# One block of quarter matmuls per step in linear attention, attended values a step later, and denominators finished on ScalarE

## The chip, the cores and the metric

The kernel runs on one NeuronCore of a Trainium2 chip. The metric is the time of one execution on the device in microseconds (us). Five engines work side by side, each through its own instructions in order: TensorE (PE in the profile; its weight loads are shown as PEld), VectorE (DVE), ScalarE (ACT), GpSimd (POOL) and SyncE (SP), which issues most transfers. They wait for one another through semaphores. TensorE writes its results to PSUM, of which the kernel uses eight banks of 128 x 512 floats.

## The reference, cut to what matters

Eight sequences of 64 tokens and width 512 go through three residual blocks: cross attention to a context of 1601 tokens, a linear-attention layer with a feed-forward part, and a mixture of eight experts. The change concerns the linear attention, with 16 heads of width 64:

```python
def _phi(x, proj):
    return jax.nn.elu(x @ proj) + 1.0
h = _ln(x, g1, beta1)
q = _phi((h @ wq).reshape(b, s, H, DH), proj)
k = _phi((h @ wk).reshape(b, s, H, DH), proj)
v = (h @ wv).reshape(b, s, H, DH)
def step(carry, qkv_t):
    kv, ksum = carry
    q_t, k_t, v_t = qkv_t
    kv = kv + k_t[..., :, None] * v_t[..., None, :]
    ksum = ksum + k_t
    num = jnp.einsum('bhd,bhde->bhe', q_t, kv)
    den = jnp.einsum('bhd,bhd->bh', q_t, ksum) + 1e-06
    return ((kv, ksum), num / den[..., None])
...
attn = jnp.moveaxis(outs, 0, 1).reshape(b, s, H * DH) @ wo
x = x + attn
h2 = _ln(x, g2, beta2)
x = x + (jax.nn.gelu(h2 @ w1 + b1, approximate=False) @ w2 + b2)
```

The scan is causal: at a token, the sums run over that token and the ones before it.

## The kernel before, in words

All is in 32-bit floats. The 512 tokens are four tiles of 128 (`NT`), each with two sequences; the width is four chunks of 128 (`KC`). Instead of the scan the kernel forms, for each sequence and head, the 64 x 64 matrix of products between key features and query features, sets to zero what lies in the future, and multiplies by the values.

The linear-attention stage works on two heads at a time, so a projection has `nj` = 8 steps `j`. For each step there are these parts:

- `linear(j, "wq")` and `linear(j, "wk")` (line 671): four matmuls of 128 x 128 weights on 512 tokens, into a PSUM bank; the trace shows each matmul as two instructions, 8 in all. ScalarE copies the bank to `lin`.
- `features(j)` (line 687): the projection of width 64, as four matmuls (8 instructions) that each use a quarter, 64 x 64, of TensorE's array, into two banks. VectorE takes the minimum with 0, ScalarE the exponential, VectorE the sum with the positive part. The result `phi` has one buffer for `wq` and one for `wk`.
- `products(j)` (line 710): 16 quarter matmuls (32 instructions) of key features by query features into two banks, which VectorE multiplies by the causal mask into `masked`.
- `attend_j(j)` (line 735): four quarter matmuls with ones for the denominators (8 instructions) and 16 with the values (32 instructions), into two banks. VectorE adds 1e-6 to the denominators (line 761), takes the reciprocal of 128 x 512 elements (line 762) and multiplies the attended values into `a_t[:, j]` (line 764).

After them `output(t, js)` (line 784) adds, for token tile t, the steps `js` to the output projection: two instructions for each j, with `a_t` as weights. Each of the four tiles has its own bank until all eight j are in. Then `join(t)` (line 813) adds the residual and takes the statistics on VectorE and a square root on ScalarE, `normal(t)` (line 824) normalizes on VectorE, and `turn_h2(t)` (line 829) transposes the tile on TensorE and evicts four chunks, by turns on VectorE and ScalarE. `hidden(f, tokens)` (line 863) is the first matmul of the feed-forward part; the kernel runs `hidden(0)` on three tiles, then turns the last tile, then goes on. GpSimd adds the second bias and the residual once a tile is normalized (lines 884, 885).

The order of every engine's work is the order in which the program writes it (`manual_schedule`, line 96). What can move are the banks: `mm_bank` (projections, products, output tiles 0 and 1, turned tiles) and `acc_bank` (features, attended values, output tiles 2 and 3) have four each, and a new use waits until an old one is read. Weights come through a ring of 12 buffers; `need` (line 209) issues transfers on SyncE's queue ahead of their use, in an order fixed at the start.

Before the change a step of the loop is, on TensorE: `linear(j, "wq")`, `features(j - 1)` with `attend_j(j - 2)`, `linear(j, "wk")`, `products(j - 1)`. So quarter matmuls stand in two blocks of each step between full matmuls of 128 x 128. After the loop come `features(7)`, then pieces of the output projection with `attend_j(6)`, `products(7)` and `attend_j(7)` between them.

Of the kernel before, what the change touches and what calls it, by code (L numbers as in the profile page):

```python
# [15 lines left out]
F32 = mybir.dt.float32  # L16
AF = mybir.ActivationFunctionType
# [3 lines left out]
P = 128  # L21
B, S, D = 8, 64, 512
LK = 1601
NT = B * S // P
# [24 lines left out]
def perceiver_kernel(  # L49
# [22 lines left out]
    nc = tc.nc  # L72
    const = ctx.enter_context(tc.tile_pool(name="const", bufs=1))
# [10 lines left out]
    def mm_bank(name):  # L84
        return ps.tile([P, 512], F32, tag="mm", name=name)

    def acc_bank(name):
        return ps.tile([P, 512], F32, tag="acc", name=name)
# [120 lines left out]
    def need(*key):  # L209
        if key[0] not in ("ctxT", "ctx", "tail", "wv"):  # L210
            done(*[k for k in held if place[k] < place[key] - AHEAD + 1])
            issue_to(place[key] + 1 + AHEAD)
        else:
            issue_to(len(order))
        return streamed[key]
# [9 lines left out]
        nc.gpsimd.memset(rows, 0.0)  # L225
    eps = const.tile([P, 1], F32, name="eps")
    nc.gpsimd.memset(eps, LN_EPS)
    warm0 = const.tile([P, 1], F32, name="warm0")
    nc.scalar.activation(warm0, eps, AF.Sqrt)
    b2_bc = const.tile([P, D], F32, name="b2_bc")  # L230
# [434 lines left out]
    if True:  # L665
        a_t = la1.tile([P, H * DH // P, B * S], F32, name="a_t")

        nj = H * DH // P
        lin, phi, qk_banks, masked, sums = {}, {}, {}, {}, {}

        def linear(j, which):


            w = need(which, j // 4)
            bank = mm_bank(f"{which}_{j}")
            for c in range(KC):
                nc.tensor.matmul(  # L677
                    bank,
                    w[:, c, (j % 4) * P : (j % 4 + 1) * P],
                    h_t[:, c, :],  # L680
                    start=(c == 0),
                    stop=(c == KC - 1),
                )
            lin[which, j] = la2.tile([P, B * S], F32, tag=f"lin_{which}", name=f"lin_{which}_{j}")
            nc.scalar.copy(lin[which, j], bank)

        def features(j):

            pr = {which: acc_bank(f"pr_{which}_{j}") for which in ("wq", "wk")}
            for r in range(2):  # L690
                rows = slice(r * DH, (r + 1) * DH)
                for which, other in (("wq", r), ("wk", 1 - r)):
                    nc.tensor.matmul(
                        pr[which][other * DH : (other + 1) * DH, :],
                        proj2[rows, :],
                        lin[which, j][rows, :],
                        start=True,
                        stop=True,
                    )

            ex = {}
            for which in pr:
                ex[which] = la2.tile([P, B * S], F32, tag="ex", name=f"ex_{which}_{j}")
                nc.vector.tensor_scalar_min(ex[which], pr[which], 0.0)
                nc.scalar.activation(ex[which], ex[which], AF.Exp)
            for which in pr:
                phi[which, j] = la2.tile([P, B * S], F32, tag=f"phi_{which}", bufs=1, name=f"phi_{which}_{j}")
                nc.vector.scalar_tensor_tensor(phi[which, j], pr[which], 0.0, ex[which], ALU.max, ALU.add)

        def products(j):  # L710


            banks_ = [mm_bank(f"qk_{j}_{r}") for r in range(2)]
            for t in range(NT):
                for h in range(2):
                    cols = slice(t * P + h * S, t * P + (h + 1) * S)
                    for r in range(2):
                        rows = slice(r * DH, (r + 1) * DH)
                        nc.tensor.matmul(
                            banks_[r][h * S : (h + 1) * S, t * S : (t + 1) * S],  # L720
                            phi["wk", j][rows, cols],
                            phi["wq", j][rows, cols],
                            start=True,
                            stop=True,
                        )
            for r in range(2):
                m = masked[j, r] = la2.tile([P, NT, S], F32, tag="masked", name=f"masked_{j}_{r}")
                nc.vector.tensor_tensor(
                    m,
                    banks_[r][:, : NT * S].rearrange("p (t q) -> p t q", t=NT),  # L730
                    mask[:, None, :].to_broadcast([P, NT, S]),
                    ALU.mult,
                )

        def attend_j(j):

            both = [acc_bank(f"nd_{j}_{h}") for h in range(2)]
            for r in range(2):  # L740
                for h in range(2):
                    nc.tensor.matmul(
                        both[h][r * DH : (r + 1) * DH, NT * S :],
                        ones[h * S : (h + 1) * S, :DH],
                        masked[j, r][h * S : (h + 1) * S, :, :].rearrange("p t q -> p (t q)"),
                        start=True,
                        stop=True,
                    )
            for t in range(NT):
                for r in range(2):  # L750
                    for h in range(2):
                        nc.tensor.matmul(
                            both[h][r * DH : (r + 1) * DH, t * S : (t + 1) * S],
                            v_sb[h * S : (h + 1) * S, t, (2 * j + r) * DH : (2 * j + r + 1) * DH],
                            masked[j, r][h * S : (h + 1) * S, t, :],
                            start=True,
                            stop=True,
                        )
            rden = la2.tile([P, 2, NT * S], F32, tag="rden", bufs=1, name=f"rden_{j}")
            for h in range(2):  # L760
                nc.vector.tensor_scalar_add(rden[:, h, :], both[h][:, NT * S :], 1e-6)
            nc.vector.reciprocal(rden, rden)  # L762
            for h in range(2):
                nc.vector.tensor_tensor(
                    a_t[:, j, :].rearrange("p (t h q) -> p t h q", t=NT, h=2)[:, :, h, :],
                    both[h][:, : NT * S].rearrange("p (t q) -> p t q", t=NT),
                    rden[:, h, :].rearrange("p (t q) -> p t q", t=NT),
                    ALU.mult,
                )

        for j in range(nj):
            linear(j, "wq")
            if j > 0:
                features(j - 1)
            if j > 1:
                attend_j(j - 2)
            linear(j, "wk")
            if j > 0:
                products(j - 1)

        wo_r = [need("wo", r) for r in range(2)]
        wo_banks = {}
# [1 line left out]
        def output(t, js):  # L784
            if t not in wo_banks:
                wo_banks[t] = (mm_bank if t < 2 else acc_bank)(f"wo_{t}")
            for j in js:
                nc.tensor.matmul(  # L788
                    wo_banks[t],
                    a_t[:, j, t * P : (t + 1) * P],  # L790
                    wo_r[j // 4][:, j % 4, :],
                    start=(j == 0),
                    stop=(j == nj - 1),
                )

        features(nj - 1)

        warm2 = small.tile([P, 1], F32, tag="warm2", name="warm2")
        nc.scalar.activation(warm2, eps, AF.Sqrt)
        output(0, range(0, 3))  # L800
        attend_j(nj - 2)
        output(0, range(3, nj - 2))
        products(nj - 1)
        output(1, range(nj - 2))
        attend_j(nj - 1)
        output(2, range(nj // 2 + 1))
        for t in range(2):
            output(t, [nj - 2, nj - 1])


        h2n, h2_t = v_sb[:, :, :D], v_sb[:, :, D:]
# [12 lines left out]
        def normal(t, mv, std):  # L824
            rstd = small.tile([P, 1], F32, tag="rstd1", name=f"rstd_h2_{t}")
            nc.vector.reciprocal(rstd, std)  # L826
            nc.vector.tensor_scalar(h2n[:, t, :], xin[:, t, :], mv[:, 0:1], rstd, ALU.subtract, ALU.mult)
# [16 lines left out]
        of = join(0), join(1)  # L844
        for t in range(2):
            normal(t, *of[t])
        output(2, range(nj // 2 + 1, nj))
        of = join(2)
        output(3, range(nj // 2))
        normal(2, *of)  # L850
        turn_h2(0)
        turn_h2(1)
        output(3, range(nj // 2, nj - 2))
        turn_h2(2)
        output(3, range(nj - 2, nj))
        of = join(3)
        normal(3, *of)
    las.close()
# [226 lines left out]
    t = NT - 1  # L1085
# [688 lines left out]
```

## Time and profile before

| what | value |
|---|---|
| time, median of 3 runs (lowest to highest) | 633.23 us (633.15 to 633.51) |
| profiled execution, whole time | 633.73 us |
| its span, first to last instruction | 632.0 us |
| mean granted TensorE clock | 0.995 |
| TensorE busy, share of the span | 616.1 us, 97% |
| VectorE busy | 182.3 us, 29% |
| ScalarE busy | 121.0 us, 19% |
| GpSimd busy | 65.0 us, 10% |
| linear attention, first projection to the last turned tile | 172.3 to 283.7 us |

Times inside the span count from its first instruction. A line of the timeline gives the start, the length from the first start to the last end, the engine, the line of the kernel, the operation with `written<-read` tiles, the shape and the number of instructions merged; in brackets stands the engine's idle time before it and what ended it. Matmuls overlap: a full one of 512 columns is shown with some 0.59 us, though the next starts 0.43 us after it, so distances of starts tell more than lengths. The tile names are those of the program: `pr` features, `qk` products, `nd` attended values and denominators, `wo` the output projection, `tr_h` turned tiles, `v_sb` (whose memory the normalized tiles reuse), `hid` the feed-forward part.

### The profile page before, as it was taken

The numbers are of one execution on the slowest core, as the hardware profiler recorded it, in microseconds if no ns is written. First come the engines' busy times: TensorE is split into PE (matmuls) and PEld (weight loads), VectorE is DVE, ScalarE is ACT, GpSimd is POOL, SyncE is SP. The second block draws the span as 40 slices with busy tenths as digits, with TensorE's granted clock in tenths as the row PEclk, the third lists the DMA queues.
The fourth block names the chain that finished last, engine by engine and source line by source line (L and its number), as shares of the span: only waits on it lengthen the run. The fifth ranks groups of instructions, "written<-read, shape, count | busy, mean of one in ns | idle before, by whom it ended". The sixth has DMA issues, their size and how long they took to land. (4 is left out here: it accounts for less than half of the span.)

```text
span 632.0 us, 8729 instructions
## 1 busy us (share of the span) xinstructions
PE 616.1 (97%) x3572; PEld 349.1 (55%) x3572; DVE 182.3 (29%) x430; ACT 121.0 (19%) x226; POOL 65.0 (10%) x88
## 2 busy tenths in 40 slices
PE   8999999999999999999999999999999999999994
PEld 6543434343444444455444446967783757775793
DVE  4122323243326888670000026511311111101100
ACT  2241323230132122031011111301101101101110
POOL 4000000000000000050000003331310121301100
PEclk9999999999999999999999999999999999999998
DMA  8999999999511203030313221437890577784711
GB/s 334 418 423 423 422 423 422 425 426 417 239 61 64 71 2 135 1 132 1 117 33 117 67 100 68 170 94 256 298 346 0 189 281 284 296 311 146 296 19 17
DMA packets 23938, 131.81 MB, mean 209 GB/s; under 512 B 4373, under 2 KB 4373, under 8 KB 12489
## 3 DMA queue, kind: packets, MB, share of 16 engines
q1 hardware_dynamic: 19496, 122.36, 49.1%
q0 software_dynamic: 3280, 7.61, 4.8%
q10 hardware_dynamic: 1104, 1.07, 0.5%
q8 instruction: 38, 0.62, 0.4%
q14 instruction: 20, 0.16, 0.1%
HBM read 126.08 MB, written 4.94 MB: 207 GB/s over the span
## 5 line engine op out<-in xcount | busy, mean ns | idle before, releaser
L1271 PEld LDWEIGHTS up<-xgT,e_up 128*128 128x128 f32 x896 | 100.7, 192 | 4.5 <-ACT y_sb L1249 2.5
L1271 PE MATMUL up<-xgT,e_up 128*128 128x128 f32 x896 | 101.6, 276 | 1.0 <-PEq L1604 0.6
L1237 DVE TENSOR_TENSOR mid<-up,act 128x256 f32<-128x256 f32 x38 | 16.2, 425 | 151.0 <-ACT act L1235 149.5
L1285 PE MATMUL y<-e_wo,mid 128*128 128x512 f32 (+1 forms) x144 | 58.8, 547 | 0.0
L869 PE MATMUL hid<-v_sb,w 128*128 128x512 f32 (+2 forms) x144 | 56.6, 545 | 0.0
L890 PE MATMUL mlp<-w,hid_sb 128*128 128x512 f32 x112 | 51.0, 597 | 0.0
L456 PE MATMUL sc<-ctxT,pw_t 128*64 128x401 f32 (+1 forms) x256 | 46.7, 503 | 0.5 <-DMA ctxT<-in_ctx_T_dram 0.5
L517 PE MATMUL av<-ctx,eT 128*64 128x512 f32 x192 | 44.5, 596 | 0.2 <-DMA ctx<-in_ctx_dram 0.2
L869 PEld LDWEIGHTS hid<-v_sb,w 128*128 128x128 f32 x144 | 26.2, 190 | 29.1 <-issue 27.2
L1235 ACT ACTIVATE act<-up 128x256 f32<-128x256 f32 x38 | 14.6, 383 | 120.4 <-PE up L1271 97.5
L1285 PEld LDWEIGHTS y<-e_wo,mid 128*128 128x128 f32 x144 | 25.7, 190 | 20.5 <-issue 17.8
L1250 POOL DMA_INDIRECT out_dram<-y_sb,dst_late x12 | 18.3, 1526 | 168.2 <-ACT y_sb L1249 99.6
L890 PEld LDWEIGHTS mlp<-w,hid_sb 128*128 128x128 f32 x112 | 20.8, 190 | 23.5 <-issue 23.4
L456 PEld LDWEIGHTS sc<-ctxT,pw_t 128*64 128x64 f32 x256 | 17.8, 136 | 27.0 <-issue 25.4
L884 POOL TENSOR_TENSOR xin<-xin,b_bc 128x512 f32<-128x512 f32 x4 | 5.1, 1268 | 267.1 <-DVE rstd_h L826 263.8
L677 PE MATMUL wk<-h_t,wk 128*128 128x512 f32 x64 | 29.5, 604 | 0.0
L677 PE MATMUL wq<-h_t,wq 128*128 128x512 f32 x64 | 29.4, 602 | 0.0
L587 PE MATMUL v<-wv,h_t 128*128 128x512 f32 x64 | 29.2, 598 | 0.0
L788 PE MATMUL wo<-wo,a_t 128*128 128x512 f32 x64 | 28.9, 599 | 0.0
L938 DVE TENSOR_TENSOR xs<-mlp,xs 128x512 f32<-128x512 f32 x3 | 2.1, 691 | 86.6 <-PE mlp L890 86.6
L762 DVE RECIPROCAL rden<-rden 128x512 f32<-128x512 f32 x8 | 26.8, 3354 | 0.3
L517 PEld LDWEIGHTS av<-ctx,eT 128*64 128x64 f32 x192 | 13.3, 136 | 24.5 <-issue 23.2
(270 smaller groups left out, 621.0 us busy)
## 6 DMA issues: line engine op xcount, KB each, us to landing
e_up<-in_L_ffn_up_dram SPq DMA_DIRECT2D x32, 1024.0 KB, 6.9
ctx<-in_ctx_dram SPq DMA_DIRECT2D x24, 1024.0 KB, 15.2
ctxT<-in_ctx_T_dram SPq DMA_DIRECT2D x24, 802.0 KB, 13.9
e_wo<-in_L_ffn_wo_dram SPq DMA_DIRECT2D x16, 1024.0 KB, 15.6
w<-in_L_attn_w_dram SPq DMA_DIRECT2D x8, 1024.0 KB, 4.7
ctxT<-in_ctx_T_dram SPq DMA_DIRECT2D x8, 796.0 KB, 17.5
wv<-in_L_attn_wv_dram SPq DMA_DIRECT2D x2, 1024.0 KB, 13.6
wq<-in_L_attn_wq_dram SPq DMA_DIRECT2D x2, 1024.0 KB, 15.3
```

The costliest lines, as they stand in the source:

```text
L456: nc.tensor.matmul(sc[h * S : (h + 1) * S, :width], pw_t[:, c, (2 * t + h) * S : (2 * t + h + 1) * S], keys[h][:, c, :], start=(c == 0), s ...
L517: nc.tensor.matmul(av[h * S : (h + 1) * S, :], e_t[:, 4 * g + j, h * S : (h + 1) * S], rows[h][:, j, :], start=(g == 0 and j == 0), stop=F ...
L587: nc.tensor.matmul(bank, h_t[:, c, t * P : (t + 1) * P], wv_n[:, c, :], start=(c == 0), stop=(c == KC - 1))
L677: nc.tensor.matmul(bank, w[:, c, (j % 4) * P : (j % 4 + 1) * P], h_t[:, c, :], start=(c == 0), stop=(c == KC - 1),)
L762: nc.vector.reciprocal(rden, rden)
L788: nc.tensor.matmul(wo_banks[t], a_t[:, j, t * P : (t + 1) * P], wo_r[j // 4][:, j % 4, :], start=(j == 0), stop=(j == nj - 1),)
L869: nc.tensor.matmul(hid_banks[f][:, tokens], w[:, c, (f % 4) * P : (f % 4 + 1) * P], h2_t[:, c, tokens], start=(c == 0), stop=(c == KC - 1),)
L890: nc.tensor.matmul(acc[t], hid[:, t * P : (t + 1) * P], need("w2", f // 4)[:, f % 4, :], start=(f == 0), stop=(f == FF // P - 1),)
L1237: nc.vector.tensor_tensor(hid, bank[:, FQ:], act, ALU.mult)
L1250: nc.gpsimd.indirect_dma_start(out=out, out_offset=bass.IndirectOffsetOnAxis(ap=dst[:n, :], axis=0), in_=y_sb[:n, :], in_offset=None, boun ...
L1271: nc.tensor.matmul(bank[:, m * P : (m + 1) * P], up_of[q][:, c, m * P : (m + 1) * P], xg_t[c], start=(c == 0), stop=(c == KC - 1),)
L1285: nc.tensor.matmul(bank[:, :width], h_t[:, j * P : (j + 1) * P], w[:, 2 * (q % 2) + j, n * width : (n + 1) * width], start=(q + j == 0), s ...
```

## The change

Each step of the loop now runs both projections first, and then one block of quarter matmuls: features of the step before, attended values of three steps before, products of two steps before. The function for attended values is split: its matmuls stay in `attend_j`, which returns its two banks, and the rest is `divide`, written after the products. The addition of 1e-6 goes from VectorE to ScalarE, as an Identity activation whose bias is a new constant tile `tiny`.

After the loop three steps' attended values are open instead of two, so the tail is written anew: features(7) shares a block with products(6), attended values 6 with products(7), and the pieces of the output projection are dealt out between the blocks differently. Output tiles 0 to 2 have all but their last two j before the last block, and tile 3 gets its first two soon after it; the Sqrt table is loaded by `warm2` after the last denominators. Later parts keep their order, with other pieces of output tile 3 between them.

```diff
+    tiny = const.tile([P, 1], F32, name="tiny")
+    nc.gpsimd.memset(tiny, 1e-6)
...
+            return both
+
+        def divide(j, both):
+
             rden = la2.tile([P, 2, NT * S], F32, tag="rden", bufs=1, name=f"rden_{j}")
             for h in range(2):
-                nc.vector.tensor_scalar_add(rden[:, h, :], both[h][:, NT * S :], 1e-6)
+                nc.scalar.activation(rden[:, h, :], both[h][:, NT * S :], AF.Identity, bias=tiny)
             nc.vector.reciprocal(rden, rden)
...
         for j in range(nj):
             linear(j, "wq")
+            linear(j, "wk")
             if j > 0:
                 features(j - 1)
+            both = attend_j(j - 3) if j > 2 else None
             if j > 1:
-                attend_j(j - 2)
-            linear(j, "wk")
-            if j > 0:
-                products(j - 1)
+                products(j - 2)
+            if j > 2:
+                divide(j - 3, both)
...
+        output(0, range(4))
         features(nj - 1)
+        products(nj - 2)
+        output(1, range(2))
+        divide(nj - 3, attend_j(nj - 3))
+        output(1, range(2, 5))
+        output(0, [4])
+        output(2, range(2))
+        both = attend_j(nj - 2)
+        products(nj - 1)
+        divide(nj - 2, both)
+        output(2, range(2, 5))
+        for t in range(3):
+            output(t, [5])
+        divide(nj - 1, attend_j(nj - 1))
         warm2 = small.tile([P, 1], F32, tag="warm2", name="warm2")
         nc.scalar.activation(warm2, eps, AF.Sqrt)
-        output(0, range(0, 3))
-        attend_j(nj - 2)
-        output(0, range(3, nj - 2))
-        products(nj - 1)
-        output(1, range(nj - 2))
-        attend_j(nj - 1)
-        output(2, range(nj // 2 + 1))
+        for t in range(3):
+            output(t, [6])
+        output(3, range(2))
         for t in range(2):
-            output(t, [nj - 2, nj - 1])
+            output(t, [7])
...
         of = join(0), join(1)
         for t in range(2):
             normal(t, *of[t])
-        output(2, range(nj // 2 + 1, nj))
+        output(2, [7])
         of = join(2)
-        output(3, range(nj // 2))
+        output(3, range(2, 5))
         normal(2, *of)
         turn_h2(0)
         turn_h2(1)
-        output(3, range(nj // 2, nj - 2))
+        output(3, range(5, nj - 1))
         turn_h2(2)
-        output(3, range(nj - 2, nj))
+        output(3, range(nj - 1, nj))
         of = join(3)
         normal(3, *of)
```

## The prediction

> **What bounds the kernel now.** I read the page's first part, then the waits, and then, for the stage that changes (172.3 to 283.7 us), the timelines of TensorE and VectorE.
>
> The page's busy line:
>
> ```profile
> PE 616.1 (97%) x3572; PEld 349.1 (55%) x3572; DVE 182.3 (29%) x430; ACT 121.0 (19%) x226; POOL 65.0 (10%) x88
> ```
>
> TensorE is the bound by share, and between 172.3 and 283.1 us it has no idle gap: time leaves this stage only if TensorE's issue gets denser, or comes in where TensorE is made to wait. TensorE's timeline (columns: start, length, then the instruction and its count):
>
> ```profile
> 246.17 0.69 PE L719 MATMUL qk<-phi_wq,phi_wk 64*64 64x64 f32 x32
> 246.68 0.59 PE L693 MATMUL pr_wq<-lin_wq,proj 64*64 64x512 f32 x1
> ...
> 247.92 2.84 PE L788 MATMUL wo<-wo,a_t 128*128 128x512 f32 x6
> 250.70 0.66 PE L742 MATMUL nd<-masked,ones 64*64 64x256 f32 x8
> 251.18 0.64 PE L752 MATMUL nd<-masked,v_sb 64*64 64x64 f32 x32
> 251.75 2.84 PE L788 MATMUL wo<-wo,a_t 128*128 128x512 f32 x6
> 254.53 0.69 PE L719 MATMUL qk<-phi_wq,phi_wk 64*64 64x64 f32 x32
> 255.15 5.42 PE L788 MATMUL wo<-wo,a_t 128*128 128x512 f32 x12
> 260.50 0.66 PE L742 MATMUL nd<-masked,ones 64*64 64x256 f32 x8
> ```
>
> Read the starts. Twelve full matmuls take 260.50 - 255.15 = 5.35 us, six take 254.53 - 251.75 = 2.78: one costs 0.429, and each run of them 0.20 over that, whatever its length. The 32 products take 0.62 when full matmuls follow (254.53 to 255.15) but 0.51 when quarter matmuls follow (246.17): 0.11 for leaving quarter work. The 32 attended values, the same shape, take 0.57, or 0.46 without the leaving, 0.05 less than the products, which begin a block. So each block of quarter work among full ones costs 0.20 + 0.11 + 0.05 = 0.36 us beside its work.
>
> Then the end of the stage, on TensorE and on VectorE:
>
> ```profile
> 261.55 14.00 PE L788 MATMUL wo<-wo,a_t 128*128 128x512 f32 x32
> ...
> 283.20 0.66 PE L832 MATMUL tr_h<-ident,v_sb 128*128 128x128 f32 x4 [0.32 <-DVE v_sb L827]
> ```
>
> ```profile
> 261.68 0.76 DVE L761 TENSOR_SCALAR rden<-nd 128x256 f32<-128x256 f32 x2 [3.52 <-PE nd L752]
> 262.47 3.35 DVE L762 RECIPROCAL rden<-rden 128x512 f32<-128x512 f32 x1
> 265.85 0.76 DVE L764 TENSOR_TENSOR a_t<-nd,rden 128x256 f32<-128x256 f32 x2
> 267.87 0.69 DVE L815 TENSOR_TENSOR xin<-wo,xin 128x512 f32<-128x512 f32 x1 [1.26 <-PE wo L788]
> ...
> 271.96 1.59 DVE L827 TENSOR_SCALAR v_sb<-xin,mv_h,rstd_h 128x512 f32<-128x512 f32 x1
> ...
> 276.18 0.40 DVE L840 TENSOR_SCALAR v_sb<-tr_h,col 128x128 f32<-128x128 f32 x1
> ...
> 279.68 0.41 DVE L840 TENSOR_SCALAR v_sb<-tr_h,col 128x128 f32<-128x128 f32 x1 [0.56 <-ACT v_sb L836]
> 280.34 0.69 DVE L815 TENSOR_TENSOR xin<-wo,xin 128x512 f32<-128x512 f32 x1 [0.26 <-PE wo L788]
> ```
>
> See a second chain. From the first residual addition (join(0), 267.87) VectorE works nearly without a break until the last normalized tile, on which TensorE waits 0.32 us at 283.20: 15.33 us, all in program order, four normalizations and three turned tiles' evictions. It has only two waits for TensorE, 0.08 us at join(1) and 0.26 at join(3). TensorE just covers this chain now. Whatever is left after join(0) cannot be shortened by packing TensorE.
>
> **The change, part by part**, summed on the profiled execution (span 632.0, 633.73 us in all, 0.50 above the median of 633.23).
>
> Fewer blocks. Before: two in each of steps 1 to 7 (the last one joined by features(7)), then attend(6), products(7), attend(7): 17. After: one in each of steps 1 to 7, then features(7) with products(6), attend(5), attend(6) with products(7), attend(7): 11. Six blocks at 0.36: -2.14. Between attended values and products inside a block the trace has no row: 0, as between denominators and values now, to 0.05 at each, the price of a block's first group. I take 0; the other end adds 0.3.
>
> features(7) today follows step 7's second projection by one block and waits for its copy (ScalarE's copy ends at 246.86; the feature matmuls take 1.24 us instead of the 0.97 that their regular 0.91 with a leaving cost comes to). Afterwards four output passes lie between: -0.27.
>
> Slack inside the loop. VectorE's work in the step from 197.78 to 207.59 is 8.01 us of 9.80 and falls by two 0.33 us additions against a step of 9.80 - 0.36 = 9.44 us; masked products and attended values now have a whole step. The features' last write must wait until products(j-2) have read the single phi buffer, about 2.4 us after the block's start, when the exponentials (ready 2.6 us after it) are hardly done: nothing. In the tail, attend(6) needs a bank that the first multiplication of divide(5) frees. From the start of step 7's block VectorE needs 3.80 (features, 240.62 to 244.42) + 0.66 (masks) + 3.39 (reciprocal) + 0.68 (multiplications) and again 2.65 (features, 249.92 to 252.57) + 0.66 + 3.39 + 0.42 = 15.65 us to it. TensorE arrives after 2.38 (the block) + 3.63 (8 matmuls) + 1.49 (features, products) + 1.91 (4 matmuls) + 1.06 (attend(5)) + 5.35 (12 matmuls) = 15.82. Hidden by 0.1; 0.2 to 0.3 if both banks are waited for.
>
> Denominators on ScalarE. The nearest rows are a 128x256 activation out of PSUM with no tile operand, 383 ns (line 1235), and one with a tile operand, 473 ns (line 1245); I take 473, as the new bias is a tile. Two, overlapped as the exponentials' rows overlap (0.03 to 0.1): 0.85 to 0.9 against VectorE's 0.75. In that step ScalarE is busy for 2.40 us of 9.80: hidden; uncovered, 0.9 a step. Line 836's Identity runs between square roots with no table load. The Sqrt table (1.28 us) now loads after the last denominators, with five us before join(0) asks for a root; uncovered it would cost 1.3. The memset of the constant is some 0.03 us of POOL's start-up, done 170 us before use; if it did delay POOL, 0.1. No DMA is moved, and the order of weight requests on SP stays.
>
> The tail's order. join(0) needs output(0, [7]). Before it TensorE now places 46 output matmuls instead of 36 (tiles 1, 2 and 3 are brought forward): 10 x 0.429 = +4.29 before join(0), and as much less after it.
>
> Waiting for the last a_t. From attend(7) to its first use lie 10 full matmuls (4.4 us with the switch) instead of 12 (261.55 to 266.81). The way through ScalarE and VectorE takes 0.12 + 0.38 + 0.47 + 0.03 + 3.39 + 0.34 + 0.41 + 0.05 = 5.2: +0.8 of waiting (0.6 with 383 ns rows; 0 if it were all hidden, which the row 265.85 excludes: today that load was ready 0.15 us before its turn).
>
> So output(0, [7]), and with it join(0), comes 4.29 - 2.14 - 0.27 + 0.8 = +2.7 us later. From join(0) on VectorE does the same instructions in the same order: 15.33 less its two waits for TensorE and their 0.08 of overlap, 14.9: -0.4. In that time TensorE has only 18 output matmuls (7.7), three turns (1.3) and the first hidden chunk (2.6), less the 1.06 us from the first one's issue to join(0), 10.6 us in all. So it must wait, by the starts worked out along both orders about 1.1, 0.6 and 2.7 us: at turns 1 and 2 and the last. After the last turn work is as before, dense on TensorE. Net: 2.7 - 0.4 = **+2.3 us**: 636.0 by the profiled execution, 635.5 by the median.
>
> One rule speaks against such waits. Row: the granted clock stood at 1.00 through TensorE's idle 1.26 us at 568.9, and in 626 to 628 it was 0.51, some 2.8 us after the last matmul (623.2). The Trainium skill's page "TensorE: Matmul & The Clock Gate", Part 1 on the HAM clock gate, says that an idle window of about 3.4 us halves the clock. By the rule a wait of 2.7 is safe and the sum stays; by the row it is at the edge, and the sum would be that of the clock rival.
>
> **The rivals.**
>
> Faster: TensorE's order alone decides. If VectorE's chain from join(0) fitted into TensorE's 10.6 us, the time would be 633.23 - 2.14 - 0.27 - 0.32 + 0.8 = 631.3. For it: TensorE's 97%. Against: 15.33 measured. It breaks even when the chain shrinks to 12.6, which would take both the stretch at 271.96 (1.59 instead of 0.55) and most of the evictions' waits for ScalarE (0.53, 0.56, 0.56).
>
> Same: the stretch at 271.96 goes. It coincides with POOL's addition at 272.00, begun 0.04 us after it. If VectorE got ahead, -1.05: 634.4. Against: both start from the preceding normalization, whose distances do not change.
>
> Slower by banks or loop waits: both banks waited for, or phi's writes, or ScalarE's place behind the exponentials, late at a few steps: +0.6 to +1.5, so 636.1 to 637.0. For it: the 0.1 us margin.
>
> Slower by the clock: in 1.4 to 3.4 us TensorE issued 9 matmuls of 128x128, 0.21 each, and later 0.109 each; 3.4 us so lose 1.7: 637.2. Decides if the third wait passes 2.8 us.
>
> The change doesn't do what it says: the 0.36 is not a matter of switching and stays in the longer block: 635.5 + 2.1 = 637.6. Against: it shows in runs of 6, 8 and 12 alike.
>
> **How the numbers follow.** VectorE's tail chain, 634.9 to 636.1: 64%. Banks or loop 9%, clock 6%, nothing saved 4%: slower in all 83%. POOL's stretch gone 7% and part (2%) of a chain shortened: within 0.2% (1.27 us, about what a measurement can tell), 9%. The rest of that short chain, faster: 8%. The range takes in the first case, banks and POOL: 634.3 to 637.0.
>
> **What would show it.** Right: steps of 9.44 us in the loop; features(7) without the 0.27; a wait of 0.6 to 1 us at the first output pass with j = 7; three waits of TensorE for normalized tiles, the last near 2.7 us; VectorE's chain from join(0) near 14.9; total TensorE idle in the stage near 5 us. Wrong: steps still near 9.8, no waits at the turns, a granted clock under 1.00 near the end of the stage, or idle time moved into the experts' part.

## The result, and the profile after

| | before | after |
|---|---|---|
| time, median (lowest to highest) | 633.34 us (633.13 to 633.64) | 637.13 us (636.75 to 637.45) |
| profiled execution; its span | 633.73; 632.0 us | 636.75; 635.0 us |
| first query projection | 172.31 us | 172.76 us |
| from there to join(0) | 95.56 us | 98.46 us |
| from there to the end of the last turn ("the stage") | 111.38 us | 113.74 us |
| from the end of the stage to the end of the span | 348.28 us | 348.53 us |

The ratio is 1.006, with a 95% interval of 1.0049 to 1.007: the change costs 3.79 us. 635.5 was forecast, with 637.0 as the upper end. The busy line of the page after:

```profile
PE 616.1 (97%) x3572; PEld 351.5 (55%) x3572; DVE 175.7 (28%) x414; ACT 127.0 (20%) x242; POOL 64.9 (10%) x89
```

TensorE has the same work in 3 us more of span. A step of the loop on TensorE's timeline after (start, length, instruction, count):

```profile
196.15 3.70 PE L679 MATMUL wq<-h_t,wq 128*128 128x512 f32 x8
199.69 3.60 PE L679 MATMUL wk<-h_t,wk 128*128 128x512 f32 x8
...
204.12 0.61 PE L744 MATMUL nd<-masked,ones 64*64 64x256 f32 x8
204.56 0.64 PE L754 MATMUL nd<-masked,v_sb 64*64 64x64 f32 x32
205.02 0.65 PE L721 MATMUL qk<-phi_wq,phi_wk 64*64 64x64 f32 x32
205.60 3.70 PE L679 MATMUL wq<-h_t,wq 128*128 128x512 f32 x8
```

The same step of the kernel before:

```profile
197.78 3.70 PE L677 MATMUL wq<-h_t,wq 128*128 128x512 f32 x8
...
207.59 3.70 PE L677 MATMUL wq<-h_t,wq 128*128 128x512 f32 x8
```

From one query projection to the next are 205.60 - 196.15 = 9.45 us, where the kernel before took 9.80 (9.81 by the two rows shown). The loop gains what was forecast, and no instruction in it waits. The same timeline at the end of the stage, with the waits in brackets:

```profile
251.47 5.42 PE L795 MATMUL wo<-wo,a_t 128*128 128x512 f32 x12
256.81 0.66 PE L744 MATMUL nd<-masked,ones 64*64 64x256 f32 x8
...
264.74 4.56 PE L795 MATMUL wo<-wo,a_t 128*128 128x512 f32 x10
270.05 5.42 PE L795 MATMUL wo<-wo,a_t 128*128 128x512 f32 x12 [0.75 <-DVE a_t L770]
275.30 0.60 PE L848 MATMUL tr_h<-ident,v_sb 128*128 128x128 f32 x4
276.84 0.63 PE L848 MATMUL tr_h<-ident,v_sb 128*128 128x128 f32 x4 [0.94 <-DVE v_sb L843]
...
279.46 0.66 PE L848 MATMUL tr_h<-ident,v_sb 128*128 128x128 f32 x4 [0.27 <-DVE v_sb L843]
...
282.32 2.85 PE L885 MATMUL hid<-v_sb,w 128*128 128x384 f32 x8 [1.34 <-DVE v_sb L856]
286.00 0.66 PE L848 MATMUL tr_h<-ident,v_sb 128*128 128x128 f32 x4 [0.83 <-DVE v_sb L843]
```

One wait of 0.32 us before has become five, 4.13 us in all, and each of them names VectorE: for the last attended values, for normalized tiles, and, at 282.32, for an eviction of a turned tile. VectorE's timeline over the same time:

```profile
271.21 0.69 DVE L831 TENSOR_TENSOR xin<-wo,xin 128x512 f32<-128x512 f32 x1 [1.22 <-PE wo L795]
...
274.45 0.55 DVE L843 TENSOR_SCALAR v_sb<-xin,mv_h,rstd_h 128x512 f32<-128x512 f32 x1
...
275.11 1.59 DVE L843 TENSOR_SCALAR v_sb<-xin,mv_h,rstd_h 128x512 f32<-128x512 f32 x1
...
281.54 0.73 DVE L856 TENSOR_SCALAR v_sb<-tr_h,col 128x128 f32<-128x128 f32 x2 [0.56 <-ACT v_sb L852]
282.83 0.41 DVE L856 TENSOR_SCALAR v_sb<-tr_h,col 128x128 f32<-128x128 f32 x1 [0.56 <-ACT v_sb L852]
283.15 0.68 DVE L831 TENSOR_TENSOR xin<-wo,xin 128x512 f32<-128x512 f32 x1
```

Its chain begins with join(0) at 271.21 and releases the last turn at 286.00, 14.79 us later (15.33 before). It has no wait for TensorE left. The normalization at 275.11 takes 1.59 us beside its neighbour's 0.55, as one did before.

The stage so explains 2.36 of the 3.79 us. The rest lies in two places that the stage's timelines don't show. The first is the input stream at the start. The page's row of transfer rates in 40 equal slices of the span, of after:

```profile
GB/s 338 420 418 418 418 419 417 420 420 406 260 60 105 28 2 134 2 132 1 85 50 131 67 99 67 168 94 233 306 357 0 179 286 281 262 349 157 280 19 17
```

And of before:

```profile
GB/s 334 418 423 423 422 423 422 425 426 417 239 61 64 71 2 135 1 132 1 117 33 117 67 100 68 170 94 256 298 346 0 189 281 284 296 311 146 296 19 17
```

In slices 2 to 9, from 16 to 143 us, it moves 417 to 420 GB/s after and 418 to 426 before, and before, the stage started 0.45 us earlier. The second is a new wait among the experts, on TensorE's timeline after:

```profile
550.75 1.98 PE L1301 MATMUL y<-e_wo,mid 128*128 128x512 f32 x4 [1.03 <-issue]
572.11 3.64 PE L1339 MATMUL up<-e_up,xgT 128*32 128x512 f32 x32 [0.43 <-ACTq L1618]
```

"issue" means that nothing in the profile explains the wait of 1.03 us. In return the wait at line 1339 has become 0.43; it was 1.26 in the kernel before, where this line is 1323:

```profile
568.86 3.64 PE L1323 MATMUL up<-e_up,xgT 128*32 128x512 f32 x32 [1.26 <-PEq L1602]
```

In these two executions the start (0.45), the stage (2.36) and the rest (0.25) make 3.06 us of span. The medians lie further apart, 3.79, because the profiled execution of before is 0.39 us above its median and that of after 0.38 below.

### The profile page after: what moved, and what is told of

Read it like the earlier page. It is cut to its first block, busy times and chain, and to the rows that moved or that the text cites. A ratio compares the mean times of both kernels' runs of the same rounds, so it can differ in the third digit from the quotient of the medians.

```text
span 635.0 us, 8763 instructions
## 1 busy us (share of the span) xinstructions
PE 616.1 (97%) x3572; PEld 351.5 (55%) x3572; DVE 175.7 (28%) x414; ACT 127.0 (20%) x242; POOL 64.9 (10%) x89
## 5 line engine op out<-in xcount | busy, mean ns | idle before, releaser
L458 PEld LDWEIGHTS sc<-ctxT,pw_t 128*64 128x64 f32 x256 | 19.3, 136 | 26.1 <-issue 23.6
```

The costliest lines, as they stand in the source:

```text
L458: nc.tensor.matmul(sc[h * S : (h + 1) * S, :width], pw_t[:, c, (2 * t + h) * S : (2 * t + h + 1) * S], keys[h][:, c, :], start=(c == 0), s ...
```

## The experiments

In what follows "before" stands near 633.3 us in every comparison (633.25 to 633.39). None of these kernels leaves work out; they change order, place, or an unused constant.

### The constant: e1_before_with_constant, e2_after_same_addresses, e5_before_with_64_bytes

The change adds a tile of 4 bytes per partition. In the program's layout it takes 32, and every buffer allocated after it moves by 32 bytes, the weight ring among them, whose rows started at multiples of 8192 bytes. The first run adds the tile to the kernel before:

```diff
+    tiny = const.tile([P, 1], F32, name="tiny")
+    nc.gpsimd.memset(tiny, 1e-6)
```

> The kernel before with only the new constant tile and its memset added; nothing reads it. It moves every buffer behind it, the weight ring among them, by 32 bytes. Theory A (the part of the loss that the tail chain doesn't account for comes from those moved buffers, into which all transfers then write less well): 634.3 to 634.8 us, the first query projection at 172.6 us or later instead of 172.3. Theory B (the rest is chance between two profiles, or the memset is free): within 0.3 us of the kernel before.

The second is the changed kernel with the constant in a second column of `eps`, for which no buffer moves:

```diff
-    eps = const.tile([P, 1], F32, name="eps")
+    both_eps = const.tile([P, 2], F32, name="eps")
+    eps, tiny = both_eps[:, 0:1], both_eps[:, 1:2]
...
-    tiny = const.tile([P, 1], F32, name="tiny")
```

> The changed kernel with the constant as second column of the tile eps, so that no buffer moves against the kernel before. Theory A (moved buffers cost 1.0 to 1.5 us): 635.6 to 635.9 us, 2.3 to 2.5 over the kernel before, and linear attention as in the changed kernel. Theory B (buffers don't matter): 637.1 us.

The third moves the buffers of the kernel before by 64 bytes:

```diff
+    wide = const.tile([P, 16], F32, name="wide")
+    nc.gpsimd.memset(wide, 1e-6)
```

> The kernel before with an unused constant of 64 bytes a partition, which moves the same buffers by 64 bytes instead of 32. With 32 bytes the time rose by 0.5 us and the packets of the input stream between 15 and 75 us took 39.74 ns per KB instead of 39.45. Theory A (what counts is where a row starts within 64 bytes): 633.4 us and 39.45 ns per KB, as the kernel before. Theory B (any move away from the old places costs, for example because the ring's rows then no longer start at multiples of 8 KB): 633.9 us and 39.74.

| run | time, us | ratio to before (95%) | stage starts | stage | ns per KB of the input stream's packets, 15 to 75 us |
|---|---|---|---|---|---|
| before | 633.3 | | 172.31 | 111.38 | 39.45 |
| before + 32 bytes | 633.88 | 1.001 (1.0001 to 1.0019) | 172.61 | 111.38 | 39.74 |
| before + 64 bytes | 633.96 | 1.0011 (1.0002 to 1.0021) | 172.78 | 111.38 | 39.78 |
| after | 637.13 | 1.006 (1.0049 to 1.007) | 172.76 | 113.74 | 39.73 |
| after, unmoved | 636.40 | 1.0049 (1.0035 to 1.0063) | 172.25 | 113.74 | 39.44 |

The transfer rates of the changed kernel with its buffers unmoved:

```profile
GB/s 339 418 422 423 422 424 422 426 426 415 227 52 114 20 1 134 2 133 0 96 45 125 67 99 67 169 94 246 295 354 0 183 284 283 269 337 164 274 19 17
```

Slices 2 to 9 are back at 418 to 426, and the stage starts where it did. The packets' price per KB goes with the place of the buffers in all five runs, and in the other kernels below too: 39.44 or 39.45 in all eleven whose buffers are unmoved. The 0.7 to 0.8% on it delays the work that the stream feeds by 0.3 to 0.5 us. In medians the place costs 0.5 to 0.7 us: 637.13 - 636.40 = 0.73 in the changed kernel, whose two intervals overlap, and 0.5 and 0.7 in the one before, whose intervals reach down to 0.1. This is less than was expected (1.0 or more), and the first two runs came out between their theories. It can be more than the delay of the stage's start; what the difference is, if it is one, was not found. That it is the multiple of 8192 that counts, and not any multiple above 64, was not tried.

### The length of TensorE's program: e8_before_16_matmuls_at_start, e9_shorter_start

The changed stage issues 16 more waits on semaphores on TensorE (132 instead of 116 in the trace), so that all its later program lies 16 instructions further on. The program comes in 16 KB packets on a queue of its own. The idle matmuls at the very start of the kernel, four instructions each, change the length and next to nothing else: in the run below the stage starts at 172.37 us instead of 172.31. In the kernel before:

```diff
-NIDLE = 12
+NIDLE = 16
```

> The kernel before with 16 instead of 12 warm-up matmuls, which run while TensorE waits for its first input, and which make its program longer by 16 instructions ahead of everything else: as many as the change adds to it, as waits. Theory (the new wait of 1.0 us at the output matmuls of an expert near 550 us is a wait for code, which moves with the place of the code): a wait of 0.5 to 1.5 us appears at those matmuls near 547 us, and the one near 569 us falls from 1.26 to about 0.4: 633.3 to 634.1 us. Rival (that wait belongs to data, or to the later time): no such wait, 633.4 us.

The time was 634.49 us (ratio 1.0019, 1.001 to 1.0028), 0.4 above the expected range; the stage 111.38. The waits of the changed kernel are there, in a kernel that has none of the change:

```profile
548.74 1.98 PE L1285 MATMUL y<-e_wo,mid 128*128 128x512 f32 x4 [1.51 <-issue]
570.42 3.64 PE L1323 MATMUL up<-e_up,xgT 128*32 128x512 f32 x32 [0.75 <-ACTq L1602]
```

The other way about, in the changed kernel (buffers unmoved):

```diff
-NIDLE = 12
+NIDLE = 8
```

> The changed kernel with its buffers unmoved, and 8 instead of 12 idle multiplications at the very start, which shortens TensorE's program ahead of all its work by the 16 instructions that the change had added to it. Theory (the wait of about 1 us at the y matmuls near 550 us is TensorE waiting for its program, whose parts fell elsewhere because of the added instructions): that wait is gone, the wait near 569 us is 0.8 to 1.3 us as in the kernel before, the stretch from the first query projection to the end of the last turn stays 113.74 us, and the time is the kernel before plus 2.36, 635.7 us. Rival (the wait belongs to the new order of the stage and not to the program's length): the wait stays and the time is 636.4 us.

It took 635.92 us (1.004, 1.0026 to 1.0054), the stage 113.74. The wait at the y matmuls is gone; the other has its old size:

```profile
571.13 3.64 PE L1339 MATMUL up<-e_up,xgT 128*32 128x512 f32 x32 [1.30 <-PEq L1618]
```

The queues' share of transfers in the changed kernel, for 548 to 549 us alone (packets, MB, share of 16 engines), has the packet just ahead of the wait:

```profile
q8 instruction: 1, 0.02, 5.5%
```

It starts at 548.32 us, takes 0.055 x 16 = 0.9 us, and TensorE goes on at 550.75, 1.55 us after it has landed; the distance is 1.4 to 1.6 us in all eight runs with such a wait. In the run with the shorter start the packet ahead of that place starts 2.4 us sooner than in the same kernel with 12 idle matmuls (545.2 for 547.6 us), and nothing waits. So the wait follows the program's length, not the new order, and all fourteen kernels of this document agree: the eight whose program on TensorE is 13 to 17 instructions longer than before have a wait of 0.9 to 1.8 us at the y matmuls, the six others have none. From the end of the stage to the end of the span the eight take 348.53 to 349.90 us, the six 347.93 to 348.35.

Between the runs with and without the wait the medians differ by 0.5 (636.40 to 635.92) and 1.2 us (634.49 to 633.3). The second difference is clear of noise. The intervals of the first overlap, and in the traces of those two runs the rest after the stage differs by 0.26 us only.

### The two halves: e3_denominators_on_vector, e11_before_scalar_adds

The new order with the additions left on VectorE:

```diff
-                nc.scalar.activation(rden[:, h, :], both[h][:, NT * S :], AF.Identity, bias=tiny)
+                nc.vector.tensor_scalar_add(rden[:, h, :], both[h][:, NT * S :], 1e-6)
```

> The changed kernel with the denominators' 1e-6 added on VectorE as before, and so without the constant tile: the new order alone. Theory (in the new tail VectorE is the bound, and 0.66 us per step returns to it): attended values of step 6 wait 1.4 us for a bank, join(0) comes 1.5 us later, 637.2 us, so 1.5 over the kernel with the same addresses. Rival (the two additions are hidden as TensorE sets the pace): no difference to that kernel.

It took 638.66 us (1.0083, 1.0069 to 1.0097), 2.26 more than the kernel with unmoved buffers where 1.5 was expected; the stage 115.21, 1.47 longer than with ScalarE. The rest is the wait for the program again, 1.78 us at the y matmuls here: after the stage the trace takes 349.72 us for 348.61. In its stage, TensorE's timeline has a wait that the changed kernel doesn't have:

```profile
257.70 0.44 PE L742 MATMUL nd<-masked,ones 64*64 64x256 f32 x3 [0.86 <-DVE a_t L768]
```

Attended values 6 wait here for the banks that the multiplications of step 5 free. The block from its first instruction to the next output pass takes 259.22 - 256.19 = 3.03 us against 258.34 - 256.81 = 1.53 in the changed kernel: that is the whole difference.

The additions on ScalarE, in the kernel before, with no buffer moved:

```diff
-                nc.vector.tensor_scalar_add(rden[:, h, :], both[h][:, NT * S :], 1e-6)
+                nc.scalar.activation(rden[:, h, :], both[h][:, NT * S :], AF.Identity, bias=tiny)
```

> The kernel before with its loop and order, and only the additions to the denominators moved to ScalarE (the constant lies in the second column of an existing tile, so no buffer moves). Theory (this half of the change is worth nothing by itself, since VectorE did not set the loop's pace): the stretch to the end of the last turn is 111.38 us within 0.2, and the time 633.3 to 633.5 us. Rival (VectorE's additions held the loop): up to 0.66 us less for each of the steps it held, so 632 us or less.

633.54 us (1.0001, 0.9992 to 1.001), the stage 111.54: 0.16 longer, and no gain. By itself this half is worth nothing; in the new order it is worth 1.5 us of the stage, because there the banks' margin is small.

### VectorE's chain: e4_evictions_on_scalar, e12_additions_reversed, e6_tail_in_other_order, e7_other_order_and_evictions

All four start from the changed kernel with its buffers unmoved (stage 113.74). If VectorE's chain from join(0) sets the end, work taken off it must shorten the stage, up to the point where another engine sets it. First, the evictions of turned tiles 0 to 2 all on ScalarE:

```diff
-                if c % 2:
+                if c % 2 or t < NT - 1:
                     nc.scalar.activation(
```

> The changed kernel with unmoved addresses, and the evictions of turned tiles 0 to 2 all on ScalarE instead of by turns with VectorE: 3.9 us leave VectorE's chain behind join(0). Theory (that chain sets the end of the stage): the last turned tile comes 2.1 us earlier than in the kernel with the same addresses, 633.5 us, and TensorE's wait at it falls from 2.2 to about 0.7 us. Rival (the time goes elsewhere, to TensorE's own order): as that kernel.

635.24 us (1.0029, 1.0017 to 1.0041), the stage 112.18: 1.56 less, where 2.1 was expected. The timelines of ScalarE and TensorE say where the rest went. ScalarE:

```profile
277.94 4.28 ACT L852 ACTIVATE v_sb<-tr_h,col 128x128 f32<-128x128 f32 x12
```

TensorE:

```profile
281.23 2.85 PE L885 MATMUL hid<-v_sb,w 128*128 128x384 f32 x8 [0.84 <-ACT v_sb L852]
```

Twelve evictions in a row last 4.28 us, and the first hidden matmul now waits for them instead of for VectorE's. Second, GpSimd's additions begin with the last tile, so that none runs beside the normalizations:

```diff
-    for t in range(NT):
+    for t in reversed(range(NT)):
         nc.gpsimd.tensor_tensor(xin[:, t, :], xin[:, t, :], b2_bc, ALU.add)
```

> The changed kernel with its buffers unmoved, and only the order of GpSimd's additions of bias and residual reversed, so that the first of them waits for the last normalization. Theory (the normalization of tile 1 takes 1.59 us because GpSimd's addition runs beside it): that normalization takes 0.55 to 0.7 us, the stretch to the end of the last turn is 112.7 us instead of 113.74, and the time 635.35 us. Rival (GpSimd is not the cause): 1.59 us stays, and the time is 636.4 us.

635.65 us (1.0038, 1.0024 to 1.0052), the stage 112.70, as expected. VectorE's timeline, the normalizations of tiles 0 and 1:

```profile
273.94 0.55 DVE L843 TENSOR_SCALAR v_sb<-xin,mv_h,rstd_h 128x512 f32<-128x512 f32 x1
274.60 0.55 DVE L843 TENSOR_SCALAR v_sb<-xin,mv_h,rstd_h 128x512 f32<-128x512 f32 x1
```

The second took 1.59 us while GpSimd's addition ran; now it takes 0.55, and the whole 1.04 us comes out of the stage. The additions cost next to nothing where they are now, from 284.5 us on: the rest after the stage is 348.72 us for 348.61.

Third, the output passes dealt out anew, with 42 matmuls of them instead of 46 ahead of the pass that join(0) needs (the expectation says 34, which is a miscount):

```diff
-        output(0, range(4))
-        features(nj - 1)
-        products(nj - 2)
...
+        output(0, [0, 1])
+        output(1, [0])
+        features(7)
+        output(1, [1])
+        products(6)
...
+        output(3, [0])
+        output(2, [5])
+        output(0, [7])
+        of[0] = join(0)
```

> The changed kernel with unmoved addresses, the same loop and the same instructions, but the tail's output passes dealt out again: 34 of them instead of 46 before the pass that join(0) waits for, and as many more behind it. Theory (what the change lost is the time at which join(0) comes, since VectorE's chain behind it is fixed): join(0) 1.8 us earlier than with the change's own tail, the waits of TensorE at the turns mostly gone, the stage 3.3 us shorter than in that kernel: 633.1 us. Rival (the new loop itself, or three open steps instead of two, is the loss): within 0.5 us of 636.4.

635.30 us (1.0032, 1.0021 to 1.0042), the stage 112.28. This missed: join(0) came 1.79 us earlier, as expected, but the stage gained only 1.46 of an expected 3.3, since the chain from join(0) took 15.12 us instead of 14.79. VectorE's normalizations of tiles 1 and 2 in this run:

```profile
274.30 1.42 DVE L819 TENSOR_SCALAR v_sb<-xin,mv_h,rstd_h 128x512 f32<-128x512 f32 x1
275.82 1.58 DVE L819 TENSOR_SCALAR v_sb<-xin,mv_h,rstd_h 128x512 f32<-128x512 f32 x1
```

GpSimd's timeline beside them:

```profile
274.17 1.27 POOL L910 TENSOR_TENSOR xs<-xs,xin 128x512 f32<-128x512 f32 x1
275.86 1.27 POOL L909 TENSOR_TENSOR xin<-xin,b_bc 128x512 f32<-128x512 f32 x1 [0.42 <-DVE rstd_h L818]
```

Two normalizations now fall beside additions instead of one. The additions end at 275.44 and 277.13, the normalizations at 275.72 and 277.40: each ends 0.27 to 0.28 us after the addition that it met. The added stretch is worth 0.87 us (1.42 for 0.55); what else the expectation had wrong is not shown. Fourth, a similar order together with the evictions on ScalarE:

```diff
+        output(0, [7])
+        output(1, [7])
+        of[0] = join(0)
+        output(2, [5])
+        output(3, [3])
+        output(2, [6])
+        normal(0, *of[0])
...
-                if c % 2:
+                if c % 2 or t < NT - 1:
```

> As the kernel with the tail in another order, and also the evictions of turned tiles 0 to 2 on ScalarE, with an order fitted to that. Theory (both halves of the loss removed, so the saved blocks reach the end): the last turned tile 4.4 us earlier than with the change's own tail and unmoved addresses, 632.0 us, about 1.4 less than the kernel before. Rival (TensorE already sets the pace once the order is mended): no gain over that kernel, 633.1.

633.01 us (0.9996, 0.9987 to 1.0005), the stage 110.20: 1.18 less than before, where 2.0 was expected. Two normalizations still took 0.93 and 0.88 us beside GpSimd, and the rest after the stage is 349.90 us instead of 348.28, with waits of 0.61 and 1.51 us for the program.

### All together: e10_best_version

The changed loop; evictions of tiles 0 to 2 on ScalarE; GpSimd's additions reversed; buffers unmoved; `NIDLE = 8`; and this tail:

```diff
+        output(0, [0, 1, 2])
+        output(1, [0])
+        features(7)
+        products(6)
+        output(0, [3])
+        output(1, [1])
+        heads[5] = attend_j(5)
+        output(1, [2])
+        output(0, [4])
+        output(1, [3])
+        divide(5, heads[5])
+        products(7)
+        heads[6] = attend_j(6)
+        divide(6, heads[6])
...
+        heads[7] = attend_j(7)
+        divide(7, heads[7])
...
+        output(0, [7])
+        output(1, [7])
+        of[0] = join(0)
+        of[1] = join(1)
+        output(2, [5, 6])
+        normal(0, *of[0])
+        output(3, [3])
+        output(2, [7])
+        turn_h2(0)
+        normal(1, *of[1])
+        output(3, [4, 5])
+        of[2] = join(2)
+        turn_h2(1)
+        output(3, [6])
+        normal(2, *of[2])
+        turn_h2(2)
+        output(3, [7])
+        of[3] = join(3)
```

> The new loop with the tail's output passes in another order, the evictions of turned tiles 0 to 2 on ScalarE, GpSimd's additions of bias and residual in reversed order of tiles (so that its first one starts only when the last normalization is done), buffers unmoved, and TensorE's program as long as in the kernel before. Theory (order of the tail, evictions behind VectorE, GpSimd stretching the normalizations, and the program's length are the four things that cost): the stretch to the end of the last turn is 109.0 to 109.4 us against 111.38 before, the normalizations take 0.55 to 0.7 us each, and the time is 630.9 to 631.3 us, faster than both kernels. Rival (the normalizations stretch for another reason, and the waits for the program do not follow its length): as in the run with other order and evictions, 633.0 us.

631.36 us, just above the expected range; the ratio is 0.9968 (0.9957 to 0.9979), faster than both kernels. TensorE's timeline at the end of its stage:

```profile
262.37 10.73 PE L795 MATMUL wo<-wo,a_t 128*128 128x512 f32 x24
272.94 0.60 PE L824 MATMUL tr_h<-ident,v_sb 128*128 128x128 f32 x4
...
277.69 2.80 PE L895 MATMUL hid<-v_sb,w 128*128 128x384 f32 x8
280.75 0.66 PE L824 MATMUL tr_h<-ident,v_sb 128*128 128x128 f32 x4 [0.26 <-DVE v_sb L819]
```

Of the five waits one of 0.26 us is left. The stage is 109.27 us, 2.11 less than before: join(0) comes 96.88 us after its start, and VectorE's chain takes 280.75 - 268.85 = 11.90 us instead of 14.79. What the loop gained was there all along; it shows only where VectorE's chain hardly delays the end. The kernel before has 0.32 us of waiting in its stage, so the same edits without the new loop could hardly give more than that; this is argued, not run.

## Why the prediction was right and wrong

The direction and the mechanism were right, and the stage's sum was right to 0.1 us, with some luck: join(0) came 0.2 us later than forecast, and VectorE's chain was 0.1 us shorter. The time was 1.6 us too low, mainly because two costs outside the stage were priced at nothing or nearly so.

- **Fewer blocks (-2.14) and features(7) (-0.27).** Right. The step is 9.45 us (9.44 forecast). join(0) comes 2.90 us later; 4.29 of brought-forward passes and a wait that is shown as 0.75, plus the 0.16 by which a full matmul's shown length exceeds its pace, make 5.20, so 2.30 were saved against a forecast 2.41. The rival that nothing would be saved is out.
- **Slack of the banks (hidden by 0.1).** Right. Nothing waits at 256.81. How thin the margin was, the run with the additions on VectorE shows: the rival's wait comes, at its upper price of 1.5 us.
- **Denominators on ScalarE (0.85 to 0.9, hidden).** Right: 0.82 to 0.84 us for two. In the kernel before they are worth nothing.
- **Waiting for the last attended values (+0.8).** 0.75.
- **join(0) +2.7; VectorE's chain 14.9.** 2.90 and 14.79: net +2.36 for a forecast +2.3. The waits at the turns were forecast as 1.1, 0.6 and 2.7 us; they are 0.94, 0.27 and then 1.34 + 0.83, so 3.38 for 4.4, and 4.13 in the whole stage for "near 5". The last one is split: I overlooked that hidden(0), ahead of the last turn, needs the evictions of tile 2, which lie in the same chain.
- **The stretch at the second normalization.** It recurred, as argued from the unchanged distances; the last section has its rule. The rival's price for its going, 1.05 us, was measured as 1.04.
- **The faster rival.** It did not occur, since the chain stayed at 14.8 us. Its break-even was 12.6 and its time 631.3; with the chain at 11.9, in another order, the best version takes 631.36.
- **The clock.** It did not fall. The busy times of TensorE, VectorE and the others for the stage after, with the granted clock near the end of the row:

```profile
172.76:286.50 113.74, 109.61 (x858) 51.61 (x857) 69.97 (x98) 33.61 (x64) 8.12 (x7) 1.00 0.19 66
```

  1.00, with 4.13 us of waits. The longest of them was 1.34 us, so neither the row's 2.8 us nor the window of about 3.4 us in the Trainium skill's "TensorE: Matmul & The Clock Gate", Part 1, was put to a test. Nor is 2.8 us a fixed delay: in the fourteen traces the clock fell 2.2 to 5.2 us after the last matmul's end.
- **The memset of the constant, "0.03 us of POOL's start-up, 0.1 if it did delay".** This term failed. It counted the instruction and not the tile: 32 bytes that move every later buffer. The runs showed 0.5 to 0.7 us in medians, and 0.3 to 0.5 us of later start in the traces. That "no DMA is moved" was true of the issues, not of where they land.
- **"After the last turn work is as before, dense on TensorE."** This step failed too. The work is the same, but the program around it is longer, and the wait for it fell in another place. In medians that is 0.5 us between the changed kernel's two lengths, 0.26 in their traces, and 1.2 between those of the kernel before.

Sum: 2.36 for the stage, 0.73 for the moved buffers, 0.48 for the program's length (636.40 - 635.92) make 3.57 of 3.79. The stage's share is firm, as are the existence and the direction of the other two; their sizes are differences of medians not much larger than the noise. The 0.2 left over are within the intervals: the kernel with neither of the two extra costs is 2.5 us above the one before by its ratio, with an interval of 1.6 to 3.4.

## What to carry to other kernels

Packing the busiest engine gains only up to the next engine's chain behind it: before moving work forward on TensorE, add up what VectorE must do from the moved point to the next hand-over, and shorten that first (order of the passes, evictions elsewhere, no GpSimd work beside it). Price a new tile by the addresses it moves and not by its memset; a free column of an existing tile moves none. With an edit of a per cent or less, compare the waits in the untouched parts too, since a program that is a few instructions longer can wait elsewhere.

## What the runs showed of the hardware

- Input packets cost 39.45 ns per KB into buffers at multiples of 8192 bytes (eleven kernels) and 39.73 to 39.78 when they lay 32 or 64 bytes further on (three). Why is open.
- TensorE can stand still for 0.6 to 1.8 us in the middle of dense work until 1.4 to 1.6 us after a 16 KB packet of its program lands; 16 more or fewer instructions hundreds of us earlier decide whether and where. The profile calls it "issue", or names an engine that has long been done. The wait of 0.8 to 1.3 us near 569 us, in the six kernels without the new one, ends 1.84 to 1.87 us after such a landing. Why it resumes that long after the landing is open.
- A VectorE normalization of 128x512 that meets a GpSimd addition of 128x512 ends 0.27 to 0.29 us after that addition, whatever is left of it: five stretched ones (1.59 in the changed kernel, 1.42, 1.58, 0.93 and 0.88 in the runs with other orders) all fit. One that meets only the last 0.2 us of an addition, as at 278.86 in the changed kernel, keeps its 0.55, and there the next addition takes 1.41 us instead of 1.26. The residual additions on VectorE, with one operand in PSUM, keep their 0.68 us beside GpSimd. The Trainium skill's "SBUF — State Buffer", section "Who interferes with whom", says that GpSimd and some VectorE instructions exclude each other for a whole instruction, the one that issues first going on. The runs agree on the blocking. They can't test the order, since the profile shows starts: at 275.11 the normalization is shown 0.04 us ahead of the addition that held it up.
